# A four-layer image network on one core: start-up loads, the last experts and small vector work put elsewhere

## The chip, the cores and the metric

The kernel runs on one core of a Trainium2 chip. The metric is the device time of one execution in microseconds (us). The core has a tensor engine (PE, with its weight loads shown as PEld), a vector engine (DVE), an activation engine (ACT), GpSimd (POOL) and SyncE (SP), which issues DMAs. Each engine runs its own instructions in order and waits on semaphores where it needs another's result.

## The reference

The input is `x`, 4 images of 384 channels by 48 x 48 positions, in float32. Four layers follow one another, each `x = x + layer(group_norm(x))`:

```python
# layer 0: a Mamba block over the 2304 positions of an image, 768 inner channels, 16 states
xz = xs @ in_proj_w.T; xin, z = split(xz)
xin = silu(causal_conv4(xin) + conv_b)
dt, B, C = split(xin @ x_proj_w.T); dt = softplus(dt @ dt_proj_w.T + dt_proj_b)
h = exp(dt * A) * h + dt * B * xin        # per position, a scan; A = -exp(A_log)
y = (h * C).sum(states) + xin * D
out = layer_norm((y * silu(z)) @ out_proj_w.T) * gamma + beta
# layer 1: 1x1 product, an 8x8 patch FFT filter, a depthwise 3x3 convolution, a gelu gate, 1x1 product
# layer 2: a depthwise 11x11 convolution whose kernels are made from 4 points per channel
# layer 3: 4 experts (two 384x384 products with a relu), each weighted by a coefficient
present = (top_i[:, :, None] == arange(e)).any(0)     # is expert e anyone's k-th choice?
coef = einsum("ke,kbhw->ebhw", present, top_w)
out = einsum("ebohw,ebhw->bohw", y, coef)
```

If every expert is somebody's first and somebody's second choice, all coefficients are 1, and the last layer is the plain sum of the experts' outputs. The kernel computes that sum, works out from the gate scores whether the case holds (`route_all`), and has a second path (`weighted`) for the other case, which these inputs don't take.

## The kernel before, in words

The group normalisations are not applied to the data. Their scale goes into the weights of the product that follows (`fold` for layer 0, `begin` and `all_experts` for the experts), and the mean, multiplied by these weights, goes into a bias (the products with a right side one column wide, `pbias` and `pb`).

**Start.** Weights are loaded by `weight` (line 418) and a few direct calls, all issued on ACT's DMA queue. On SP's queue go three constants, then image 0, one channel tile of 128 x 2304 at a time, whose moments DVE takes by `bn_stats`, six to a tile (lines 477 to 481). `group_norm` makes mean and reciprocal deviation. Some small tables follow (`filt_t` by the product `fps`; `band`, layer 2's points as a matrix, made by DVE on lines 519 to 535), then `fold(0, 0)` and `fold(0, 1)` (x's half and z's half of the input weights), the load of the first chunk `xch`, which takes memory that the start's tiles held, and its products `pin`.

**Scans.** `scans` goes over 20 chunks (4 images of 5 chunks of about 460 positions), each of 96 slots. In a slot stands one scan over one channel tile and one state (`scan`, line 844), with its decay on ACT (`decay`), its drive on POOL (`drive`), the product with C on DVE or, in every third slot, on POOL, and the sum over states as transposes into PSUM on PE (`turned`, line 770). The whole order of this stage is written out (`manual_schedule`).

All other work is put beside these scans as tasks: generators whose every `yield` names an engine and may name a condition. A `Lane` holds tasks and moves each by one step in a slot; `Meter` lets only so much tensor work into a slot. `aux` holds layer 0's own work, placed by `plan` at slots given in numbers (`put(66, ...)`); `one` holds layers 1 to 3 of the image before (`later`), and `two` the experts of that image (`experts`), 16 blocks of 144 positions for each of 4 experts. A block is two groups of nine matrix products (`ph`, `pout`) with a relu on ACT between and an addition on DVE behind. Once in a chunk, at slot 64, `gates` runs Silu over a whole chunk for x and z, with a change of ACT's tables before and after it; the decays of later slots wait behind that. `image_stats` takes the moments of the next image in halves of three `bn_stats`. In layer 1 the depthwise convolution is 27 taps on DVE for each of 6 strips of an image, in `finish_strip`, two to three in a slot.

**Tail.** After the last scan, `one` runs layers 1 to 3 of the last image while `two` finishes the experts of the image before. Then `route_all` works the routes out of all scores, a chain of some 50 small DVE operations, and `all_experts` runs the four experts on the last image with all their weights in memory: it loads and scales the weights, makes the biases by `pb`, and goes over 16 blocks of positions. Outside the written-out stage a scheduler may move instructions past one another where the data allow it.

Of the kernel before, what the change touches and what calls it, by code (L numbers as in the profile page):

```python
# [9 lines left out]
F32 = mybir.dt.float32  # L10
# [129 lines left out]
def tile_layers(ctx: ExitStack, tc: tile.TileContext, a: dict, out: bass.AP):  # L140
# [272 lines left out]
    with ExitStack() as first:  # L413
        wp = first.enter_context(tc.tile_pool(name="weights", bufs=1))
        x1d = [dram.tile([C, HW], F32, name=f"x1d{b}") for b in range(NB)]
        x2d = [dram.tile([C, HW], F32, name=f"x2d{b}") for b in range(NB)]

        def weight(name, shape, src):
            t = wp.tile(shape, F32, name=name)
            nc.scalar.dma_start(t, src)  # L420
            return t
# [6 lines left out]
        conv_s = wp.tile([P, MT], F32, name="conv_s")  # L428
        nc.vector.tensor_reduce(conv_s, conv_w, AX.X, ALU.add)

# [4 lines left out]
        w_dt = wp.tile([DTR + 1, DI], F32, name="w_dt")  # L435
        nc.scalar.dma_start(w_dt[:DTR, :], a["L0_dt_proj_wT"])
        nc.scalar.dma_start(w_dt[DTR : DTR + 1, :], a["L0_dt_proj_b"].unsqueeze(0))
        a_neg = weight("a_neg", [P, MT, DS], per_channel(a["L0_A_log"]))
        nc.scalar.activation(a_neg, a_neg, AF.Exp)
        nc.vector.tensor_scalar_mul(a_neg, a_neg, -1.0)  # L440
        w_out0 = weight("w_out0", [P, MT, C], per_channel(a["L0_out_proj_wT"]))
# [21 lines left out]
        for e in range(NE):  # L463
            nc.scalar.dma_start(b1_all[:, e, :], column(a["L3_b1"][e]))
            nc.scalar.dma_start(b2_all[:, e, :], column(a["L3_b2"][e]))
        b2_sum = wp.tile([P, CT], F32, name="b2_sum")
        nc.vector.tensor_reduce(b2_sum, b2_all.rearrange("p e c -> p c e"), AX.X, ALU.add)

# [3 lines left out]
        with (  # L472
# [69 lines left out]
        edges = [sum(BANDS[:k]) for k in range(len(BANDS) + 1)]  # L542

        ordered = [False]

# [9 lines left out]

        def scans(wk, mm, ring, meter, place, lanes, begin):

# [24 lines left out]
            def fold(b, which):  # L582
                w = (w_inx, w_inz)[which]
                d = batch[b]
                nc.sync.dma_start(
                    w, per_channel(a["L0_in_proj_wT"])[:, :, bass.ts(which, DI)]
                )
                yield from wait(5)
# [389 lines left out]
            def plan(i, at):  # L978
# [9 lines left out]
                if i:  # L988
# [59 lines left out]
            now(fold(0, 0))  # L1048
            now(fold(0, 1))
            now(load(0))  # L1050
# [65 lines left out]
        def slow_slot():  # L1116
            return place[0] % (2 * DS) % 3 == 0

        def later(b, ring, accr):
# [124 lines left out]
            def finish_strip(hb):  # L1244
# [7 lines left out]
                def taps(ct):  # L1252
                    yield ("dve", 0, (accr, 1))
                    acc, k = sums[ct] = accr.take(f"dw{b}_{hb}_{ct}")
                    v = acc[:, :LB].rearrange("p (h w) -> p h w", w=W)
                    room = 3 if slow_slot() else 2
                    for k in range(9):
                        if not room:
                            yield ("dve",)
                            room = 3 if slow_slot() else 2  # L1260
                        room -= 1
# [277 lines left out]
        def experts(b, ring, rings):  # L1539
# [54 lines left out]
            def block(s, e):  # L1594
# [68 lines left out]
        def all_experts(b, wk, banks):  # L1663
# [25 lines left out]
            )  # L1689
            xs, hs, o = {}, {}, {}  # L1690

            def load3(s):
# [45 lines left out]
            for i, (s, e) in enumerate(order):  # L1738
# [9 lines left out]
        place = [0]  # L1748

# [35 lines left out]
        with (  # L1785
# [3 lines left out]
            holder[0] = mm  # L1789
            scans(wk, mm, ring, meter, place, [one, two], begin)  # L1790
            held, two.queue = two.queue, []
            at = place[0]
            while not all(ring.read):
# [6 lines left out]
        with (  # L1800
# [3 lines left out]
            holder[0], ring.n, accr.n = mm, 6, 2  # L1804
            of_experts(wk, {"we": 2, "xe": 3, "ye": 3, "hr": 3})

            one.queue += later(NB - 1, ring, accr)
            while one.queue or one.active or two.queue or two.active:
                at += 1
                meter.slot(0.0)  # L1810
                if not (one.queue or one.active):
                    meter.value = 0.0
                for act in (True, False):
                    for lane in (one, two):
                        lane.step(act, at)
            coef, whole = route_all(rt, mm)
            all_experts(
                NB - 1, wk,
                lambda tag, name: mm.tile(
                    [P, 512], F32, name=name, tag=tag, bufs=6 if tag == "mm" else 2  # L1820
                ),
            )

# [112 lines left out]
```

## Time and profile before

| what | us |
|---|---|
| median of 3 runs (5466.89 to 5471.5) | 5467.04 |
| the profiled execution | 5472.59 |
| its span | 5470.3 |
| first scan begins at | 88.66 |
| PE busy | 4689.8 |
| DVE busy | 4176.4 |
| POOL busy | 3124.6 |
| ACT busy | 2999.9 |

The costliest groups on the page (line, engine, operation, out<-in, count, busy us and mean ns, idle time ahead and its cause):

```profile
L844 DVE TENSOR_TENSOR_SCAN da<-da,carry,bu 128x460 f32<-128x460 f32 (+1 forms) x1008 | 1182.5, 1173 | 69.9 <-ACT da L820 48.7
L864 DVE TENSOR_TENSOR g<-da,C 128x460 f32<-128x460 f32 (+1 forms) x1260 | 796.4, 632 | 87.1 <-DMA C<-bcd 28.1
L1601 PE MATMUL pout<-hr,we 128*128 128x144 f32 x3456 | 488.9, 298 | 49.7 <-ACT hr L1617 30.5
L1266 DVE SCALAR_TENSOR_TENSOR dw<-pad,w_dw,dw 128x384 f32<-128x384 f32 x576 | 347.6, 614 | 17.4 <-ACT pad L1241 6.5
```

How to read it: PE shows two records for each float32 product. Busy time is an average over stages with different limits, so a stage's own row (busy time of each engine within it) says more than a share of the whole. A wait is put down to what came last. Idle time of an engine that isn't the bottleneck costs nothing.

### The profile page before, as it was taken

To read this page: it belongs to the slowest core of one execution; us is meant where nothing else is said; L and a number is where in the kernel's file an instruction comes from. 1 tells how busy PE (TensorE), PEld (TensorE's weight loads), DVE (VectorE), ACT (ScalarE), POOL (GpSimd) and SP (SyncE) were. 2 spreads that over 40 slices of the span, in tenths; PEclk is the share of its full clock that TensorE was granted. 3 is DMA by queue.
4 is the path that set the end of the run, shared out by engine and by line. 5 is a ranking of instruction groups with operands and counts; after the bars stand their busy time and mean duration, and the time that the engine had idled before them with its cause. 6 is when DMAs were issued, how large, how long until landed. Compare 5 with 4: busy or idle time off the path is not lost. (4 is left out here: it accounts for less than half of the span.)

```text
span 5470.3 us, 82006 instructions
## 1 busy us (share of the span) xinstructions
PE 4689.8 (86%) x27796; PEld 3688.4 (67%) x27796; DVE 4176.4 (76%) x5806; ACT 2999.9 (55%) x6632; POOL 3124.6 (57%) x2795
## 2 busy tenths in 40 slices
PE   5677677777678989988899999988899999999899
PEld 3445445454447767665678887665678878888799
DVE  5889989999898898899988788899988774443200
ACT  3555555565458765655467655665566753334321
POOL 3878878865567777665567667665666662000000
PEclk8788888798789999999899999999999999999899
DMA  4445445454345555544566566554556564543200
GB/s 121 135 137 147 124 128 146 128 149 124 104 125 148 151 160 163 172 140 140 152 169 174 155 166 175 153 154 130 164 158 169 163 175 145 148 138 102 66 27 23
DMA packets 628393, 758.97 MB, mean 139 GB/s; under 512 B 58869, under 2 KB 622181, under 8 KB 627582
## 3 DMA queue, kind: packets, MB, share of 16 engines
q1 hardware_dynamic: 617668, 751.98, 48.5%
q8 instruction: 221, 3.62, 0.3%
q10 hardware_dynamic: 10298, 1.67, 0.2%
q14 instruction: 206, 1.69, 0.1%
HBM read 663.81 MB, written 89.65 MB: 138 GB/s over the span
## 5 line engine op out<-in xcount | busy, mean ns | idle before, releaser
L831 POOL TENSOR_TENSOR bu<-u,B 128x460 f32<-128x460 f32 (+1 forms) x1920 | 2226.4, 1168 | 1118.2 <-DVE g L844 506.7
L820 ACT ACTIVATE da<-dt,a_neg 128x460 f32<-128x460 f32 (+1 forms) x1920 | 1243.7, 649 | 317.3 <-DVE g L864 223.0
L770 PE MATMUL y<-ident,g 128*115 128x128 f32 (+1 forms) x7680 | 1169.0, 295 | 273.4 <-DVE g L864 202.0
L770 PEld LDWEIGHTS y<-ident,g 128*115 128x115 f32 (+1 forms) x7680 | 1024.1, 185 | 546.9 <-DVE g L864 246.8
L844 DVE TENSOR_TENSOR_SCAN da<-da,carry,bu 128x460 f32<-128x460 f32 (+1 forms) x1008 | 1182.5, 1173 | 69.9 <-ACT da L820 48.7
L873 POOL TENSOR_TENSOR g<-g,C 128x460 f32<-128x460 f32 (+1 forms) x660 | 767.7, 1163 | 197.9 <-ACT carry L858 195.9
L864 DVE TENSOR_TENSOR g<-da,C 128x460 f32<-128x460 f32 (+1 forms) x1260 | 796.4, 632 | 87.1 <-DMA C<-bcd 28.1
L844 DVE TENSOR_TENSOR_SCAN g<-da,carry,bu 128x460 f32<-128x460 f32 (+1 forms) x528 | 616.8, 1168 | 105.6 <-ACT da L820 61.1
L858 ACT COPY carry<-da 128x1 f32<-128x1 f32 x1008 | 159.0, 158 | 948.1 <-DVE g L864 944.8
L1601 PE MATMUL pout<-hr,we 128*128 128x144 f32 x3456 | 488.9, 298 | 49.7 <-ACT hr L1617 30.5
L1601 PEld LDWEIGHTS pout<-hr,we 128*128 128x128 f32 x3456 | 461.1, 199 | 70.2 <-ACT hr L1617 40.6
L1601 PE MATMUL ph<-xe,we 128*128 128x144 f32 x3456 | 471.1, 292 | 15.2 <-DMA xe<-x3d 10.1
L1601 PEld LDWEIGHTS ph<-xe,we 128*128 128x128 f32 x3456 | 448.6, 195 | 30.4 <-DMA xe<-x3d 8.9
L1408 PE MATMUL pc<-band,row 128*128 128x162 f32 (+14 forms) x3456 | 456.2, 285 | 7.1 <-ACT row L1395 7.1
L1408 PEld LDWEIGHTS pc<-band,row 128*128 128x128 f32 x3456 | 443.5, 195 | 11.0 <-ACT row L1395 8.3
L642 PE MATMUL pin<-xch,w_inx 128*128 128x463 f32 (+2 forms) x720 | 332.5, 602 | 33.4 <-DMA xch<-in_x 20.0
L1266 DVE SCALAR_TENSOR_TENSOR dw<-pad,w_dw,dw 128x384 f32<-128x384 f32 x576 | 347.6, 614 | 17.4 <-ACT pad L1241 6.5
L915 PE MATMUL po<-w_out,zs 128*115 128x384 f32 (+1 forms) x960 | 342.4, 497 | 9.3 <-DVE dt L750 7.8
L674 PE MATMUL pinz<-xch,w_inz 128*128 128x460 f32 (+1 forms) x720 | 326.3, 592 | 0.3 <-DVE ye L1633 0.3
L1617 ACT ACTIVATE hr<-ph,nb 128x144 f32<-128x144 f32 x576 | 176.2, 376 | 268.2 <-PE ph L1601 267.8
L844 DVE TENSOR_TENSOR_SCAN da<-da,nil,bu 128x460 f32<-128x460 f32 x252 | 294.8, 1170 | 12.8 <-ACT carry L858 8.5
L1375 ACT ACTIVATE rep<-x,br,wr 128x192 f32<-128x192 f32 x576 | 274.1, 540 | 21.0 <-DVE br L1345 20.9
(202 smaller groups left out, 5725.4 us busy)
## 6 DMA issues: line engine op xcount, KB each, us to landing
B<-bcd SPq DMA_DIRECT2D x768, 230.0 KB, 3.5
C<-bcd SPq DMA_DIRECT2D x768, 230.0 KB, 3.8
B<-bcd SPq DMA_DIRECT2D x192, 232.0 KB, 3.7
C<-bcd SPq DMA_DIRECT2D x192, 232.0 KB, 4.0
xe<-x3d SPq DMA_DIRECT2D x192, 216.0 KB, 2.9
ye<-y3d SPq DMA_DIRECT2D x144, 216.0 KB, 2.8
y3d<-ye SPq DMA_DIRECT2D x96, 216.0 KB, 2.2
xs<-x1d SPq DMA_DIRECT2D x24, 576.0 KB, 4.9
```

The costliest lines, as they stand in the source:

```text
L642: nc.tensor.matmul(ps[:, lo : halo + n], lhsT=w_inx[:, k, bass.ts(j, P)], rhs=c["x"][:, k, lo : halo + n], start=k == 0, stop=k == CT - 1,)
L674: nc.tensor.matmul(ps[:, :n], lhsT=w_inz[:, k, bass.ts(j, P)], rhs=c["x"][:, k, DCONV - 1 : DCONV - 1 + n], start=k == 0, stop=k == CT - 1,)
L770: nc.tensor.matmul(c["y", m][:w, bass.ts(k, P)], lhsT=src[:, bass.ts(k, w)], rhs=ident, is_transpose=True, start=c["terms", m] == 1 and k ...
L820: nc.scalar.activation(da[:, :n], c["dt", p][:, m % 2, :n], AF.Exp, scale=a_neg[:, m, s : s + 1])
L831: nc.gpsimd.tensor_mul(bu[:, :n], c["u", p][:, m % 2, :n], live["B", u // 2][:, :n])
L844: nc.vector.tensor_tensor_scan(here[:, :n], da[:, :n], bu[:, :n], last if t else nil[:, 0:1], ALU.mult, ALU.add,)
L864: nc.vector.tensor_mul(live["g", u][:, :n], live["h", u][:, :n], live["C", u // 2][:, :n])
L873: nc.gpsimd.tensor_mul(g[:, :n], g[:, :n], live["C", u // 2][:, :n])
L915: nc.tensor.matmul(ps[:w, :C], lhsT=c["zs"][:, m, bass.ts(k, w)], rhs=w_out0[:, m, :], start=m == 0, stop=m == MT - 1,)
L1266: nc.vector.scalar_tensor_tensor(v, src, w_dw[:, ct, k : k + 1], v, ALU.mult, ALU.add)
L1408: nc.tensor.matmul(d["acc2"][0][:, : BANDS[k] * W].rearrange("p (h w) -> p h w", w=W)[:, lo - edges[k] : hi - edges[k], xlo:xhi], lhsT=d[" ...
L1601: nc.tensor.matmul(ps[:, bass.ts(m, EB)], lhsT=w[:, k, bass.ts(m, P)], rhs=of[:, k, :], start=k == 0, stop=k == CT - 1,)
```

## The change

Six things are done at once.

1. **Start.** `weight` and the other calls only note the loads. Image 0 goes first on SP's queue, in half tiles, then x's input weights, then all noted loads, now on SP's queue too. The sums and the exponential that need loaded weights stand behind the image's moments. z's weights are loaded, scaled and multiplied by the mean no longer before the first chunk but as a task at slot 4 of it.
2. **Moments.** The second half of each moments task is loaded from slot 56 on, not 66, and its three `bn_stats` go together into the gate's slot or the one after it.
3. **Taps.** In these two slots five taps may go, not two or three.
4. **Expert results.** In `experts`, one slot more lies between the second group of products and DVE's addition.
5. **Last experts.** `all_experts` becomes a generator in parts: all eight weight loads at the start of the tail; scaling, `pb` and bias when lane `one` is empty; 4 of the 16 blocks; then `route_all`; then the rest.
6. **Held tasks.** The last 24 tasks of lane `two` (a load and a block each) wait until lane `one` is empty.

```diff
+        loads = []
         def weight(name, shape, src):
             t = wp.tile(shape, F32, name=name)
-            nc.scalar.dma_start(t, src)
+            loads.append((t, src))
             return t
...
-                nc.sync.dma_start(t, a["x"][0, bass.ts(ct, P), :])
+                for h in range(2):
+                    part = bass.ts(h, HW // 2)
+                    nc.sync.dma_start(t[:, part], a["x"][0, bass.ts(ct, P), part])
                 for k in range(6):
                     nc.vector.bn_stats(stats0[:, 0, ct, k // 3, k % 3, :], t[:, bass.ts(k, LB)])
+            nc.sync.dma_start(w_inx, per_channel(a["L0_in_proj_wT"])[:, :, :DI])
+            for t, src in loads:
+                nc.sync.dma_start(t, src)
+            nc.vector.tensor_reduce(conv_s, conv_w, AX.X, ALU.add)
+            nc.scalar.activation(a_neg, a_neg, AF.Exp)
+            nc.vector.tensor_scalar_mul(a_neg, a_neg, -1.0)
+            nc.vector.tensor_reduce(b2_sum, b2_all.rearrange("p e c -> p c e"), AX.X, ALU.add)
...
+        def gated():
+            return gated_at[0] <= place[0] <= gated_at[0] + 1
...
                 yield from wait(6)
+                if h:
+                    yield ("dve", 0, None, lambda: gated())
                 for k in range(3):
-                    yield ("dve",)
+                    if not h:
+                        yield ("dve",)
                     nc.vector.bn_stats(stats0[:, b % 2, ct, h, k, :], t[:, bass.ts(k, LB)])
...
             def gates(i, j):
                 yield ("act",)
+                gated_at[0] = place[0]
...
+                if i == 0:
+                    put(4, ("fold", 0, 1), lambda: fold(0, 1))
...
-                            put(66, ("stats", b, t, 1), lambda: image_stats(b + 1, t, 1),
+                            put(56, ("stats", b, t, 1), lambda: image_stats(b + 1, t, 1),
...
             now(fold(0, 0))
-            now(fold(0, 1))
             now(load(0))
...
+        def room_for_taps():
+            return 5 if gated() else 3 if slow_slot() else 2
...
                 if s == NS - 1:
                     done(("w", e))
+                yield from wait(1)
                 yield ("dve",)
...
             for e in range(NE):
                 nc.sync.dma_start(w1[:, e], per_channel(a["L3_w1T"][e]))
                 nc.sync.dma_start(w2[:, e], per_channel(a["L3_w2T"][e]))
+            yield
+            for e in range(NE):
                 for k in range(CT):
                     nc.scalar.activation(
                         w1[:, e, k, :], w1[:, e, k, :], AF.Copy, scale=rstd3[:, b, k : k + 1]
                     )
...
             xs, hs, o = {}, {}, {}
+            yield
...
                 if i:
                     output(*order[i - 1])
+                if (s, e) == (4, 0):
+                    yield
             output(*order[-1])
+            yield
...
-            at = place[0]
+            at = place[0] + 1
...
+            last = all_experts(
+                NB - 1, wk,
+                lambda tag, name: mm.tile(
+                    [P, 512], F32, name=name, tag=tag, bufs=6 if tag == "mm" else 2
+                ),
+            )
+            next(last)
             one.queue += later(NB - 1, ring, accr)
+            ended = False
             while one.queue or one.active or two.queue or two.active:
                 at += 1
                 meter.slot(0.0)
                 if not (one.queue or one.active):
                     meter.value = 0.0
+                    if not ended:
+                        ended = True
+                        next(last)
+                held = [] if ended else two.queue[-24:]
+                two.queue = two.queue[: len(two.queue) - len(held)]
                 for act in (True, False):
                     for lane in (one, two):
                         lane.step(act, at)
+                two.queue += held
+            next(last)
             coef, whole = route_all(rt, mm)
-            all_experts(...)
+            next(last)
```

More of the change, by code (lines that the diff above doesn't have):

```diff
@@ L428, in tile_layers @@
         conv_s = wp.tile([P, MT], F32, name="conv_s")
-        nc.vector.tensor_reduce(conv_s, conv_w, AX.X, ALU.add)
         w_x = weight("w_x", [P, MT, XR], per_channel(a["L0_x_proj_wT"]))
@@ L435, in tile_layers @@
         w_dt = wp.tile([DTR + 1, DI], F32, name="w_dt")
-        nc.scalar.dma_start(w_dt[:DTR, :], a["L0_dt_proj_wT"])
-        nc.scalar.dma_start(w_dt[DTR : DTR + 1, :], a["L0_dt_proj_b"].unsqueeze(0))
+        loads.append((w_dt[:DTR, :], a["L0_dt_proj_wT"]))
+        loads.append((w_dt[DTR : DTR + 1, :], a["L0_dt_proj_b"].unsqueeze(0)))
         a_neg = weight("a_neg", [P, MT, DS], per_channel(a["L0_A_log"]))
-        nc.scalar.activation(a_neg, a_neg, AF.Exp)
-        nc.vector.tensor_scalar_mul(a_neg, a_neg, -1.0)
         w_out0 = weight("w_out0", [P, MT, C], per_channel(a["L0_out_proj_wT"]))
@@ L463, in tile_layers @@
         for e in range(NE):
-            nc.scalar.dma_start(b1_all[:, e, :], column(a["L3_b1"][e]))
-            nc.scalar.dma_start(b2_all[:, e, :], column(a["L3_b2"][e]))
+            loads.append((b1_all[:, e, :], column(a["L3_b1"][e])))
+            loads.append((b2_all[:, e, :], column(a["L3_b2"][e])))
         b2_sum = wp.tile([P, CT], F32, name="b2_sum")
-        nc.vector.tensor_reduce(b2_sum, b2_all.rearrange("p e c -> p c e"), AX.X, ALU.add)
         stats0 = wp.tile([P, 2, CT, 2, 3, 6], F32, name="stats0")
@@ L542, in tile_layers @@
         edges = [sum(BANDS[:k]) for k in range(len(BANDS) + 1)]
+        place = [0]
+        gated_at = [-9]
+        def gated():
+            return gated_at[0] <= place[0] <= gated_at[0] + 1
         ordered = [False]
@@ L554, in now, with scans @@
                 pass
-        def scans(wk, mm, ring, meter, place, lanes, begin):
+        def scans(wk, mm, ring, meter, lanes, begin):
             G = [(b, t) for b in range(NB) for t in range(NC)]
@@ L584, in fold @@
                 d = batch[b]
-                nc.sync.dma_start(
-                    w, per_channel(a["L0_in_proj_wT"])[:, :, bass.ts(which, DI)]
-                )
+                if b or which:
+                    nc.sync.dma_start(
+                        w, per_channel(a["L0_in_proj_wT"])[:, :, bass.ts(which, DI)]
+                    )
                 yield from wait(5)
@@ L1255, in taps @@
                     v = acc[:, :LB].rearrange("p (h w) -> p h w", w=W)
-                    room = 3 if slow_slot() else 2
+                    room = room_for_taps()
                     for k in range(9):
@@ L1259, in taps @@
                             yield ("dve",)
-                            room = 3 if slow_slot() else 2
+                            room = room_for_taps()
                         room -= 1
@@ L1743, in all_experts @@
                     output(*order[i - 1])
+                if (s, e) == (4, 0):
+                    yield
             output(*order[-1])
+            yield
         rings = {}
         holder = [None]
-        place = [0]
         def of_experts(pool, sizes):
@@ L1789, in tile_layers @@
             holder[0] = mm
-            scans(wk, mm, ring, meter, place, [one, two], begin)
+            scans(wk, mm, ring, meter, [one, two], begin)
             held, two.queue = two.queue, []
-            at = place[0]
+            at = place[0] + 1
             while not all(ring.read):
@@ L1805, in tile_layers @@
             of_experts(wk, {"we": 2, "xe": 3, "ye": 3, "hr": 3})
+            last = all_experts(
[3 more added lines that the diff above has]
+                ),
+            )
+            next(last)
             one.queue += later(NB - 1, ring, accr)
+            ended = False
             while one.queue or one.active or two.queue or two.active:
@@ L1815, in tile_layers @@
                         lane.step(act, at)
+                two.queue += held
+            assert ended
+            next(last)
             coef, whole = route_all(rt, mm)
[L1817 to L1822, printed above, removed]
+            next(last)
         flag = nc.values_load(whole[0:1, 0:1], min_val=0, max_val=1)
```

## The prediction

> **What bounds the kernel now.** I read the page first, then busy time by stage (windows cut where the first scan starts, where a layer's work begins, and at the tail), then the vector engine's waits, then the timelines of start and tail.
>
> ```profile
> PE 4689.8 (86%) x27796; PEld 3688.4 (67%) x27796; DVE 4176.4 (76%) x5806; ACT 2999.9 (55%) x6632; POOL 3124.6 (57%) x2795
> 88.00:1250.00 1162.00, 842.70 (x3744) 569.86 (x3745) 1053.02 (x1309) 673.20 (x1424) 941.74 (x841) 0.82 0.48 136
> 2700.00:3400.00 700.00, 667.25 (x4415) 552.61 (x4414) 581.12 (x779) 452.12 (x996) 473.36 (x417) 0.97 0.60 168
> 3900.00:4545.00 645.00, 607.01 (x4094) 506.77 (x4093) 524.23 (x683) 415.56 (x922) 432.31 (x381) 0.97 0.60 170
> ...
> 4559.00:4985.00 426.00, 406.35 (x2734) 352.20 (x2732) 177.74 (x354) 123.79 (x304) 3.19 (x12) 0.98 0.48 138
> 5123.90:5180.70 56.80, 35.55 (x159) 23.28 (x159) 15.95 (x56) 9.93 (x19) 0.54 (x1) 0.72 0.22 67
> 5180.70:5470.30 289.60, 283.90 (x2305) 283.68 (x2305) 17.79 (x62) 59.31 (x193) 0.00 (x0) 0.99 0.09 24
> ...
> DVE ye L1633 <- PE pout L1601: 85.4, 56, 3.8
> DVE g L844 <- ACT da L820: 67.2, 21, 8.2
> ...
> DVE xe L1636 <- PE pout L1601: 15.4, 15, 2.6
> ...
> 32.28 0.42 DVE L535 TENSOR_TENSOR band<-band,insidex 128x252 f32<-128x252 f32 x1
> 32.84 0.37 SPq L624 DMA_DIRECT2D xch<-in_x  x1
> ...
> 55.82 0.27 ACT L651 ACTIVATE pin<-nil,wm 128x3 f32<-128x3 f32 x1 [16.68 <-PE pin L642]
> ...
> 5164.90 0.59 PE L316 MATMUL pseen<-seen,ones 128*128 128x8 f32 x2 [12.89 <-DVE seen L310]
> 5165.34 15.50 PE L1678 MATMUL pb<-mean,w 128*128 128x1 f32 x72
> 5180.70 6.06 PE L1701 MATMUL ph<-xf,w 128*128 128x144 f32 x36
> ```
>
> A stage line gives length, then busy time of PE, PEld, DVE, ACT, POOL, clock share, DMA share, GB/s. The first scan stage is DVE's (1053.02 of 1162, 91%); where experts run beside scans it is PE's (95% and 94%). After the scans (about 4559 to 5470.3, 911 us) PE is the bound but for 5123.9 to 5180.7, where it is busy 35.55 of 56.8 us. The wait lines (total, times, longest; scans alone, 88 to 4540) show two kinds of DVE idleness that the change touches: the gates (ACT spends 1.28 + 2.50 + 2.49 + 1.28 = 7.5 us on table loads and Silu, and scans wait for `da`), and expert results not yet there (85.4 + 15.4 us).
>
> **What the Trainium skill says.** "TensorE: Matmul & The Clock Gate", part 1 on the HAM clock gate: half clock is the default, full clock needs a busy window of about 3.4 us, an idle one takes it back. The trace agrees: 72 passes of `pb` took 15.50 us at 5165 (0.215 each) after 12.89 us of waiting, 18 at 2316 took 2.09 us (0.116). "DMA: Bandwidth & Descriptors", "Anatomy of one DMA": [...]waits on semaphores are done by the issuing sequencer, so one blocked issue holds all behind it; the trace has a median of 2.4 us for the 1.5 KB `b_all` loads, and `xch` issued only 0.14 us after `band` ended. Same page, "Queues, rings and completion order": descriptors are consumed in ring order; no stage here shows eight large loads ahead of urgent ones, so that part is an estimate.
>
> **The change, part by part** (against the profiled span, 5470.3 us; that execution took 5472.59, the median of the runs shown is 5467.04, so a difference on the span is put on 5467).
>
> *Image first, z later.* Image data arrives at about 400 GB/s in both. Before, `a_neg` (issued at 4.38 us, used at 16.84) stood in DVE's order amid the moments, which ended at 22.4; with the weights behind, moments end near 14.5, 8 us earlier. But in the new instruction order 25 loads and 14 small ones stand on SP's queue ahead of `xch`, at 0.42 to 0.5 us an issue, each reusing the completion slot of the eighth before it; `w_out` waits for `w_inx` (about 15.5 us), `w_gate` for `w_out` (about 20.5), so `fsel` lands near 28.5. `fps` is ahead of x's bias products on PE: they run 30.2 to 38.2 (before 36.26 to 43.2), `cb` ends at 39, and DVE makes `band` only afterwards, by 41.8. `xch` waits for `band`, as before, so it is issued 9 us later and lands at 46.8 (5 us, as the 576 KB `xs` takes 4.9). First `pin`, three cold pairs of 1.54 us: 51.6 instead of 55.82, since z's bias products (7 us of PE amid the first `pin`) are gone. Gain 4.2 us, ends -1 and +9. z's fold then falls on the first scans: three scalings hidden under ACT's slack; 36 passes, cold, 7.8 us of PE, with `nwm` one slot behind on DVE and the scans queued after it. The fold at 802 us, as cold, shows what that costs: `nwm` waited 4.22 us. Cost 4.5 (0 to 7). Sum: **0**.
>
> *Moments and taps at gates.* Nine second-half moment groups (3 x 0.533 = 1.6 us) move to the slot after a gate, where DVE idles about 5 us; 14.4 us in all. Their load goes from slot 66 to 56 and lands (4.9 us) before. Worth full value where DVE is the bound, less at the rest: -11. Taps: in the new order only one gate gets more (+3 taps, but its gap was 0.8 us), while another loses its five (3.1 us) because the work drifts. Together **-9** (-14 to 0).
>
> *One slot more before DVE takes an expert's result.* 77 of the 101 us of waits lie in the two stages where PE is 94 to 95% busy: there DVE only waits for something else. Of the remaining 24 us I take a quarter, **-6** (-24 to +3). The price is a PSUM bank held one slot longer: in the new order seven expert products (18 passes, 2.25 us each) and one fold (2 us) fall behind the last scan. That takes 18 us of PE from stages where PE is mostly the bound; I count **-14** there (-18 to -4) and **+18** in the tail.
>
> *Tail.* Routing leaves PE's path: `pb` follows the last score transpose at 5152.0 instead of 5165.3, still at full clock. Such narrow products do not hold it (the fold at 956 us slows after some 23 passes), so about 30 x 0.112 + 42 x 0.213 = 12.3 us: end at 5164.3 instead of 5180.7, **-16.4** (-21 to -12). The scaling stays on ACT beside the scores, as now (done at 5137.2). The eight weight loads (4.7 MB) now stand ahead of all tail loads, by 4625 us; at 400 GB/s 12 us in which experts get no data but for two blocks already there (9 us). PE already idles 6 us in that place; I add **+3** (0 to 10). The last 24 tasks (12 blocks, with one in flight 25 products, 56 us) move from under layer 1 of the last image to behind `pb`. Layer 1 keeps 13 to 16 products between strips, against 15 to 19, 30 us or more, where a strip's 27 taps need 27 x 0.61 = 16.5 us of DVE: covered but for about **+2**.
>
> Sum: 0 - 9 - 6 - 14 + 18 - 16.4 + 3 + 2 = **-22.4 us**, so 5467.0 - 22.4 = **5445**.
>
> **Rivals.** (1) *The extra slot frees much more*: PE idles 33 of 700 and 38 of 645 us in the expert stages, and if decoupling fills over half of it, that entry is -45, giving 5406. For it: the long total of those waits. Against: PE's own waits there are mostly on Silu, `hr` and DMA. (2) *It comes to nothing*: scans go at DVE's pace after all, so taking PE work away gives -4 and the slot gives 0, and the eight loads cost 10: 0 - 9 - 4 + 18 - 16.4 + 10 + 2 = about 0, 5467. For it: DVE is at 87% or more in most chunks that lose products. (3) *Slower*: layer 1 of the last image goes at its own chain's pace. Then 426 us do not shrink when 18 net products (25 held, 7 added) leave it, and the held ones are pure addition: +40 for what I cost at nothing, sum +17.6, 5485. It decides from 23 us on. For it: each strip is a long chain over ACT, DVE and PE, and its end is already uncovered (PE idles near 4980). Against: PE is 95% busy there and DVE 42%.
>
> **How the numbers follow.** Forecast 0.56, rivals 0.14, 0.17, 0.13. What a measurement can tell from no change is 0.2%, 11 us. Forecast's own range, from its parts, 5430 to 5460. Faster: 0.9 x 0.56 + 0.14 + a bit of rival 2 = 0.67; same: the rest of the forecast and most of rival 2, 0.18; slower: rival 3 and an edge of rival 2, 0.15. The range, 5405 to 5475, leaves out most of rival 3 and the edge of rival 1.
>
> **What would show it.** Right: first scan near 84 us with `xch` issued near 42; gates with three moments in the gap; fewer expert waits of DVE; seven products more after the last scan; `pb` right behind the score transposes, 11 to 13 us long; no routing wait on PE. Wrong: a first scan at 78 or 92; a gap of over 10 us on PE near 4630; layer 1 of the last image still 420 us long; the last scan still near 4551 us.

## The result, and the profile after

The changed kernel takes 5476.21 us (median of 20 runs, 5465.54 to 5487.94), the kernel before 5467.6 in the runs beside it. The ratio is 1.0016, with a 95% interval from 1.001 to 1.0023: 9 us more, where 22 less had been forecast. That is under the 0.2% which the prediction called no change, and just above its range.

The busy times of the whole span, on the page's first table, hardly differ from before (PE 4689.8, DVE 4176.4); the work is the same and only its place is another.

```profile
PE 4677.3 (85%) x27796; PEld 3684.2 (67%) x27796; DVE 4175.0 (76%) x5806; ACT 2996.3 (55%) x6632; POOL 3124.6 (57%) x2795
```

The stage table of the changed kernel, cut at the same events as before (columns as there). The seventh row is new: the held experts, behind `pb`.

```profile
88.00:1250.00 1162.00, 847.68 (x3779) 577.17 (x3780) 1053.99 (x1310) 674.79 (x1427) 940.48 (x840) 0.82 0.47 137
2700.00:3400.00 700.00, 656.37 (x4237) 534.32 (x4236) 585.43 (x776) 448.91 (x984) 476.07 (x420) 0.96 0.58 166
3900.00:4545.00 645.00, 611.27 (x4161) 514.91 (x4160) 530.75 (x692) 416.40 (x925) 437.55 (x385) 0.97 0.59 169
4547.70:4939.70 392.00, 363.33 (x2381) 308.68 (x2380) 171.34 (x346) 115.41 (x276) 3.20 (x12) 0.97 0.47 137
4939.70:5079.50 139.80, 133.04 (x1106) 132.01 (x1107) 21.14 (x41) 93.34 (x216) 0.54 (x1) 0.95 0.28 84
5079.50:5121.20 41.70, 33.90 (x158) 21.66 (x157) 4.33 (x18) 9.49 (x18) 0.53 (x1) 0.76 0.30 92
5121.20:5182.60 61.40, 58.81 (x453) 57.73 (x453) 19.95 (x53) 12.54 (x41) 0.00 (x0) 0.97 0.43 116
5182.60:5473.20 290.60, 284.61 (x2324) 284.39 (x2322) 17.36 (x60) 59.21 (x193) 0.00 (x0) 0.99 0.09 24
```

The last `y` product ends at 4547.7 instead of 4562.3, 14.6 us earlier (in these two profiles). From there to the end, the tail, it takes 925.5 us instead of 908.0. So the scans gained half of the 29 us forecast for them, and the tail gave back more than that: 17.5 us instead of 6.6.

DVE's waits within the scans, 88 to 4540 us (total, times, longest):

```profile
DVE da L863 <- ACT da L839: 79.9, 101, 3.3
DVE g L863 <- ACT carry L877: 56.7, 18, 8.2
DVE g L863 <- ACT da L839: 55.6, 31, 6.3
DVE da L863 <- ACT carry L877: 38.8, 33, 3.6
...
DVE ye L1657 <- PE pout L1624: 14.9, 14, 2.0
```

Before, three of them that the prediction does not show:

```profile
DVE g L844 <- ACT carry L858: 50.7, 13, 6.2
DVE da L844 <- ACT da L820: 50.5, 63, 3.2
...
DVE da L844 <- ACT carry L858: 25.3, 29, 2.2
```

The waits for expert results fell as expected (`ye` from 85.4 us in 56 waits). The four for the scans' own operands grew in sum, from 193.7 to 231.0 us, though `g` on `da` fell (67.2 before). About half of what stood behind an expert's product now stands behind something else.

The timeline of the start:

```profile
29.34 0.33 SPq L498 DMA_DIRECT2D fsel<-in_c_fsel  x1
31.36 1.62 PE L500 MATMUL fps<-fsrc,fsel 40*128 40x384 f32 x2 [9.97 <-DMA fsel<-in_c_fsel]
44.43 0.42 DVE L542 TENSOR_TENSOR band<-band,insidex 128x252 f32<-128x252 f32 x1
44.98 0.38 SPq L642 DMA_DIRECT2D xch<-in_x  x1
...
54.00 0.27 ACT L669 ACTIVATE pin<-nil,wm 128x3 f32<-128x3 f32 x1 [10.90 <-PE pin L660]
...
87.40 1.17 DVE L863 TENSOR_TENSOR_SCAN g<-da,nil,bu 128x460 f32<-128x460 f32 x1 [2.01 <-POOL bu L850]
```

`xch` waits for `band` and is issued 12 us later than before; the first scan is 1.3 us earlier. The routing has left PE's path: `pb` follows the last score transpose directly.

```profile
5106.71 0.34 PE L1541 MATMUL pgt<-ident,sc 4*128 4x4 f32 x3 [0.45 <-ACT sc L1535]
5106.98 14.26 PE L1704 MATMUL pb<-mean,w 128*128 128x1 f32 x72
5121.10 6.79 PE L1624 MATMUL ph<-xe,we 128*128 128x144 f32 x36
```

### The profile page after: what moved, and what is told of

Same layout as the page of the kernel before. It is cut to its first block, busy times and chain, and to the rows that moved or that the text cites. A ratio compares the mean times of both kernels' runs of the same rounds, so it can differ in the third digit from the quotient of the medians.

```text
span 5473.2 us, 82031 instructions
## 1 busy us (share of the span) xinstructions
PE 4677.3 (85%) x27796; PEld 3684.2 (67%) x27796; DVE 4175.0 (76%) x5806; ACT 2996.3 (55%) x6632; POOL 3124.6 (57%) x2795
## 5 line engine op out<-in xcount | busy, mean ns | idle before, releaser
L1624 PE MATMUL ph<-xe,we 128*128 128x144 f32 x3456 | 487.5, 298 | 42.6 <-DMA xe<-x3d 22.2
L1624 PEld LDWEIGHTS ph<-xe,we 128*128 128x128 f32 x3456 | 462.4, 200 | 60.7 <-DMA xe<-x3d 17.5
L660 PE MATMUL pin<-xch,w_inx 128*128 128x463 f32 (+2 forms) x720 | 333.6, 604 | 52.7 <-DMA xch<-in_x 14.7
```

The costliest lines, as they stand in the source:

```text
L660: nc.tensor.matmul(ps[:, lo : halo + n], lhsT=w_inx[:, k, bass.ts(j, P)], rhs=c["x"][:, k, lo : halo + n], start=k == 0, stop=k == CT - 1,)
L1624: nc.tensor.matmul(ps[:, bass.ts(m, EB)], lhsT=w[:, k, bass.ts(m, P)], rhs=of[:, k, :], start=k == 0, stop=k == CT - 1,)
```

## The experiments

Times are medians, and ratios are to the kernel before on the same chip, whose median was 5466.6, 5468.5, 5469.1, 5467.7 and 5469.2 us in the five sets. A single profile can be off by some 10 us over the scans: the last `y` of tail_only, whose scans are those of before, ends 11 us earlier than before's. The tail is steadier: 904 to 909 us in the seven kernels whose tail is that of before. So totals are taken from the medians, whose ratios are good to 4 to 8 us, and the profiles are read for where a difference lies. Chunks are compared from the first scan of one to the first of the next.

### Each part alone in the kernel before

**start_only**

```diff
-            nc.scalar.dma_start(t, src)
+            loads.append((t, src))
...
+            for t, src in loads:
+                nc.sync.dma_start(t, src)
...
+                    put(4, ("fold", 0, 1), lambda: fold(0, 1))
```

> The kernel before with only the start changed (image ahead of the weights on one queue, z's fold four slots into the scans). Theory P (the prediction's sum): 0 us, first scan near 84 us. Theory N (the parts give back what they gain): 0 to +4 us, xch issued near 45 us instead of 32.8, first scan near 87, and z's bias products standing in the first scans. Time P 5467, N 5467 to 5471.

5478.66 us, ratio 1.0019 (1.0012 to 1.0026): 12 us lost, where both theories had 4 at most. `xch` is issued at 44.92 and the first scan begins at 87.1, as theory N has it.

**gate_only**

```diff
+                if h:
+                    yield ("dve", 0, None, lambda: gated())
...
+            return 5 if gated() else 3 if slow_slot() else 2
```

> The kernel before with only the moments and taps put at the gates. Theory P: -9 us, 5458. Theory N: the gaps of the gates close by only about 1.3 us each, nine of them, and part of that comes back as other waits of DVE: -3 to -5 us, 5462 to 5464, scans of chunks 0 to 2 shorter by about 1.3 us each.

5485.64 us, 1.0033 (1.0021 to 1.0045). Both theories miss, in sign too: 19 us lost. Up to chunk 6 its profile is ahead of before's; chunks 7 to 9 are 23 us longer.

**slot_only**

```diff
+                yield from wait(1)
                 yield ("dve",)
                 key = ("y" if e else "x", s, e)
```

> The kernel before with only the one slot more between an expert's second product and DVE's taking of it. Seven products fall behind the last scan. Theory P: -6 -14 +18 = -2 us, 5465; last scan near 4531. Theory N: DVE's removed waits for pout come back as waits for the scans' own operands, so the scans gain only what the seven products took of PE, 8 us or less, and the tail grows by 15 to 18: +7 to +10 us, 5474 to 5477; last scan near 4543.

5450.86 us, 0.9969 (0.9958 to 0.9979): 16 us gained, far outside both. In the profile the last `y` ends 20.9 us earlier (11.2 in slot_and_tail, whose scans are the same), and the tail, with seven products more in it, is 905.1 us against 908.0.

**tail_only**

```diff
+            next(last)
...
+                held = [] if ended else two.queue[-24:]
+                two.queue = two.queue[: len(two.queue) - len(held)]
...
             coef, whole = route_all(rt, mm)
+            next(last)
```

> The kernel before with only the tail changed (last weights loaded and scaled early, pb ahead of routing, 24 tasks held back behind layer 1). Theory P: -16.4 +3 +2 = -11.4 us, 5456; layer 1 of the last image (last y to the last strip's pb) near 366 us against 421.8. Theory N: layer 1 shrinks by about 30 us less what the held products (26 of 2.25 us) cost behind it, so the hold loses 20 to 28 and the route and pb gain 16 to 20: 0 to +10 us, 5467 to 5477.

5492.02 us, 1.0049 (1.0035 to 1.0063): 25 us lost, the largest loss so far and outside both theories. Layer 1 of the last image did shrink, from 421.8 to 396.6 us, but behind `pb` 61.9 us of held experts follow. Within layer 1 PE now waits for the strips, 20.5 us where it was 1.9:

```profile
PE pb L1294 <- DVE act L1288: 20.5, 2, 10.6
```

### The gates taken apart

**moments_only** (`if h: yield ... gated()` and the load at slot 56) and **taps_only**:

```diff
-                    room = 3 if slow_slot() else 2
+                    room = room_for_taps()
```

> The kernel before with only the second half's moments put at the gates; TensorE's order is the one of before. Theory P: -11 us, 5456 (against 5466.6). Theory T (the loss of gate_only comes from the taps, whose drift brings 13.5 us of layer 2's products forward into chunks 7 to 9): -7 to -9 us here, 5458 to 5460, and no chunk longer than before. Theory M (the loss is the moments', which crowd the slots behind the gates where layer 1 or 2 is running): +15 us or more, 5482.

> The kernel before with only the taps' room at a gate changed (five where two or three were). Theory P: +2 us. Theory T: chunks 7 to 9 longer by 20 to 24 us together, 5486 to 5495. Theory M: within 3 us of before, 5464 to 5470.

moments_only: 5465.58, 0.9999 (0.9991 to 1.0007), nothing that can be told from none. taps_only: 5502.06, 1.0055 (1.0042 to 1.0068), 34 us lost. Theory T holds for the cause; its forecast for the moments was too good, and the one for the taps too small. At a gate itself the moments are free, as the timeline of DVE shows. Before:

```profile
206.51 1.16 DVE L844 TENSOR_TENSOR_SCAN g<-da,nil,bu 128x460 f32<-128x460 f32 x1
...
210.65 0.64 DVE L864 TENSOR_TENSOR g<-da,C 128x460 f32<-128x460 f32 x1
216.89 1.17 DVE L844 TENSOR_TENSOR_SCAN g<-da,nil,bu 128x460 f32<-128x460 f32 x1 [5.61 <-ACT carry L858]
```

In the changed kernel:

```profile
209.19 1.17 DVE L863 TENSOR_TENSOR_SCAN g<-da,nil,bu 128x460 f32<-128x460 f32 x1
...
211.34 1.45 DVE L590 BATCH_NORM_STATS2 stats<-xs 128x6 f32<-128x384 f32 x3
...
214.51 0.64 DVE L883 TENSOR_TENSOR g<-da,C 128x460 f32<-128x460 f32 x1
219.58 1.18 DVE L863 TENSOR_TENSOR_SCAN g<-da,nil,bu 128x460 f32<-128x460 f32 x1 [4.43 <-ACT carry L877]
```

From the scan shown first to the one behind the gap it takes 10.4 us in both. The gap shrinks by 1.2 us, which is what three moments in a row take of DVE's time (their records overlap their neighbours'), so nine such groups are 11 us at best. What that is worth depends on the slots that they leave. In chunks 1 and 2, where DVE is busy for 91% of the time, the eight kernels with the moments moved take 3.5 us less on average than the eleven others: the forecast's full worth of two groups. In chunks 5 to 7 and 10 to 12 moments_only is only 1.3 and 1.2 us below the mean of the six kernels whose order there is that of before.

The taps are more curious: one gate takes three taps more (chunk 6), and chunks 7 to 9 become longer. The stage rows of chunks 7 to 9 and 10 to 12, cut at the scans. Before:

```profile
1505.09:2147.79 642.70, 557.69 (x3281) 424.50 (x3281) 573.61 (x762) 427.91 (x900) 468.24 (x414) 0.92 0.52 149
2147.79:2905.51 757.72, 665.51 (x3825) 513.41 (x3826) 667.74 (x950) 437.71 (x1007) 470.41 (x422) 0.93 0.55 156
```

taps_only:

```profile
1501.67:2173.44 671.77, 588.75 (x3452) 456.25 (x3453) 574.25 (x775) 429.35 (x911) 469.54 (x415) 0.90 0.49 146
2173.44:2928.50 755.06, 662.73 (x3755) 511.05 (x3754) 663.08 (x937) 437.80 (x1003) 467.40 (x419) 0.93 0.54 156
```

Layer 2 starts 4 scans earlier and the experts behind it 21: 171 more passes of PE (the records that it shows, two for a product; 3452 less 3281) within the same 288 scans, all of them experts'. The stretch is 29.1 us longer (theory T had 20 to 24), PE's busy time 31.1, DVE's 0.6; PE's idle time, 85 us before, is 83. Chunks 7 to 9 take 665 to 672 us in all six kernels with the taps' edit and 637 to 650 in the thirteen others. By chunk 16 all that work has been given back in the order, and the time has not: chunks 13 to 19 have 100 passes fewer and are 10 us longer (1655.4 against 1644.9). Work pulled forward cost its full time; work then missing gave none back.

### The tail taken apart

**tail_no_hold** is tail_only with the lines of `held` removed; **slot_and_tail** is the same with `yield from wait(1)`.

> The kernel before with the tail's change but nothing held back: experts run under layer 1 as before, the last weights load early, pb stands ahead of the routing. Theory H (the 26 held products are nearly free under layer 1, and the hold alone makes the tail lose): pb right behind the last score transpose, -13 to -16 us, 5451 to 5454. Theory P (held products cost the same in both places): -11 us plus the early weights' +3, as with the hold: 5490 if the loads or the route are what costs in tail_only.

> The kernel before with one slot more ahead of DVE's taking of an expert's result, and the tail's change without the hold. Theory H: the two add up, -16 -14 = -30 us, 5437. Theory P: no better than the slot alone, 5451, because the seven products that fall into the tail leave nothing uncovered for the route to give.

tail_no_hold: 5463.18, 0.9991 (0.9983 to 0.9999), between its theories; slot_and_tail: 5449.46, 0.9963 (0.9949 to 0.9976), theory P's time. So the hold is what makes tail_only lose, but route and `pb` bring 5 us, not 15, and with the slot almost nothing. PE's waits in layer 1 of the last image (4551.1 to 4967.0) in slot_and_tail show why:

```profile
PE ph L1601 <- DMA xe<-x3d: 14.0, 2, 13.2
PE pout L1601 <- ACT hr L1617: 9.0, 18, 0.8
```

In slot_only the first of these is 2.9 us, and layer 1 takes 402.1 us against 415.9 here. The eight weight loads stand on the queue ahead of the experts' blocks, which theory P did not have in mind.

**slot_moments_late_tail** tests that: slot, moments and tail without hold, with the loads behind the layers.

```diff
+            yield
             for e in range(NE):
                 nc.sync.dma_start(w1[:, e], per_channel(a["L3_w1T"][e]))
                 nc.sync.dma_start(w2[:, e], per_channel(a["L3_w2T"][e]))
-            yield
-            for e in range(NE):
                 for k in range(CT):
```

> The kernel before with one slot more ahead of DVE's taking of an expert's result, the second half's moments at the gates, and routing behind pb; nothing held, the last weights loaded behind the layers as before. Theory H (the eight early loads were what took the route's gain in slot_and_tail): slot -16, moments -1 to -4, route and pb -13 to -15, together 5433 to 5438. Theory U (in the tail the seven extra products take the place of what the route gives): 5447 to 5451.

5430.54 us, 0.9933 (0.992 to 0.9946): theory H, 2 us below its range, and faster than both kernels. It has the moments too; its tail alone is 14 us shorter (888.8 against 902.6 us). Its wait for `xe` in layer 1:

```profile
PE ph L1612 <- DMA xe<-x3d: 1.8, 3, 0.8
```

### The start taken apart

**z_fold_only** moves only z's fold (`put(4, ...)`); **start_tables_first** has on SP's queue the image, x's input weights, two small loads and then the tables, and the other weights on ACT's queue, where they run beside the image again:

```diff
+            for t, src in loads[:2]:
+                nc.sync.dma_start(t, src)
...
+            for t, src in loads[2:]:
+                nc.scalar.dma_start(t, src)
```

> The kernel before with only z's fold put four slots into the scans; all loads as before. Theory P (the prediction's terms): first pin 2 to 4 us earlier, 4.5 us lost in chunk 0: within 3 us of before. Theory Z (z's 36 narrow products and its scalings in chunk 0 are the 6 to 12 us that start_only lost): 5473 to 5478, and chunks 0 and 1 longer by 4 us.

> The kernel before with the image first, z's fold four slots into the scans, but the tables that band and fps need ahead of the weights, and the weights on ACT's queue as before. Theory Q (SP's queue of 39 loads ate the gain of the early image): xch issued near 32 us, first pin near 38, first scan near 81, that is 6 us or more earlier than in the changed kernel; 5471 if z's fold costs what start_only lost. Theory B (another chain, band's or cb's on DVE, is no earlier anyway): first scan within 2 us of 87.

z_fold_only: 5464.72, 0.9997 (0.9989 to 1.0005), near theory P; its first scan is at 80.9, 7.8 us earlier than before, since x's bias products are no longer followed by z's. The fold then costs about what was forecast (4.5 us): chunk 0 takes 182.4 to 184.1 us in the seven kernels with it and 177.9 to 181.0 in the twelve without, 4.2 us less on average. start_tables_first: 5480.27, 1.0016 (1.0008 to 1.0024), first scan at 84.0. Both theories on it miss: `xch` was issued at 41.90, for `band` stood behind `cb` on DVE, and `cb` behind `fps` and `pbias` on PE. The loads were not the whole of it. (The image's moments end at 20.7 us here, at 15.6 in the changed kernel and at 22.4 before.) With the image ahead on SP's queue both kernels lose 11 to 12 us (9 to 10 by the ratios) though their first scan is 1.5 and 4.6 us earlier than before. Against z's fold alone it is 6.2 and 3.1 us later. Where the rest goes is not settled: start_only's chunks differ from z_fold_only's by no more than those of two profiles of one order do.

### Parts taken out of the changed kernel

**after_no_taps** has the old `room`, **after_no_hold** no `held`, **after_no_start** the old start.

> The changed kernel with only the taps' room set back to what it was before. Theory T (the taps' drift is the single largest loss of the change): chunks 7 to 9 shorter by 20 to 25 us than in the changed kernel, last scan near 4520, 5450 against 5476. Theory I (what the taps cost, the other parts give back whatever the taps do): 5470 or more.

> The changed kernel without the 24 held tasks. Theory H (the hold loses 25 to 30 us wherever it stands): 5446 to 5451 against 5476. Theory P (held products cost the same in both places): 5476 or more.

> The changed kernel with the start of before (weights on ACT's queue, z's bias ahead of the scans). Theory S (image first loses about 10 us everywhere, as in start_only and start_tables_first): 5464 to 5468. Theory N (it is lost in what follows): within 4 us of 5476.

after_no_taps 5468.85, 1.0001 (0.9993 to 1.001): 7 us better than the changed kernel, within the noise of theory I. Its chunks 7 to 9 are 25 us shorter, as theory T has it, but its chunks 13 to 19 are 20 us longer. after_no_hold 5450.76, 0.9964 (0.995 to 0.9977): 25 us better, theory H. after_no_start 5468.9, 1.0004 (0.9996 to 1.0013): 7 us better, a little less than theory S.

The tail of after_no_hold (layer 1; layer 2; scores and `pb`; the last image):

```profile
4552.70:4970.10 417.40, 391.81 (x2650) 340.54 (x2648) 175.60 (x352) 122.75 (x300) 3.19 (x12) 0.98 0.48 140
4970.10:5126.20 156.10, 155.04 (x1303) 153.43 (x1303) 24.61 (x47) 97.60 (x231) 0.54 (x1) 1.00 0.31 93
5126.20:5166.80 40.60, 33.38 (x158) 20.63 (x157) 4.34 (x18) 9.49 (x18) 0.53 (x1) 0.75 0.31 94
5166.80:5457.20 290.40, 284.44 (x2307) 284.22 (x2307) 29.78 (x100) 59.73 (x194) 0.00 (x0) 0.99 0.08 23
```

Here the 26 products are in layers 1 and 2, which take 573.5 us together; with them held it is 531.8, and 61.4 follow. Held, they cost 61.4 - 41.7 = 20 us more. Layers 1 and 2 had 35 us of idle PE without them and 27 with them, and PE's busy time there grew by only 50.5 us for 466 passes, where 453 behind `pb` take 58.8 and leave 2.6 us idle. So of the 20 us some 9 are gaps no longer filled, 8 are busy time that the passes take more by themselves, and 3 are new gaps.

### What the slot is worth, and why the taps cost less beside it

**products_out** moves eight products behind the last scan by another means:

```diff
-                yield ("pe", 2.2, (ring, 1), lambda: rings["hr"].free())
+                yield ("pe", 2.4, (ring, 1), lambda: rings["hr"].free())
...
-                yield ("pe", 2.2, (ring, 1))
+                yield ("pe", 2.4, (ring, 1))
```

> The kernel before with the weight of an expert's product in the meter 2.4 instead of 2.2: eight products fall behind the last scan, DVE takes a result as early as before. Theory M (what the slot gains is the work that leaves the scans for a tail that has room for it): -12 to -18 us, 5451 to 5457, with DVE's waits for pout still near 85 us. Theory W (the slot's gain is the removed waits of DVE): no gain, 5467 to 5475.

5486.69 us, 1.0036 (1.0024 to 1.0049): 19 us lost, more than theory W had (no gain), and the opposite of theory M: moving work behind the last scan does not gain by itself. With 18 us of PE less in the scans its last `y` ends 0.4 us later than before's, and its tail is 921.5 us long against 908.0. DVE's wait for results is still there (88 to 4540 us):

```profile
DVE ye L1633 <- PE pout L1601: 77.4, 49, 4.5
```

In slot_only it isn't (1490 to 4540 us, in which all such waits lie):

```profile
DVE ye L1634 <- PE pout L1601: 11.9, 13, 1.9
```

The two do not move the same products: the weight spaces all experts anew, and takes its eight mostly from chunks 13 to 15, the slot its seven mostly from chunks 10 to 12. So the place that they leave could be what counts. The rows of chunks 10 to 12 speak against that. In slot_only:

```profile
2149.68:2888.30 738.62, 651.62 (x3737) 502.30 (x3737) 663.29 (x948) 434.47 (x1000) 470.57 (x422) 0.93 0.54 157
```

That is 88 passes fewer than before and 19 us less. In taps_only it is 70 passes fewer and 3 us less. All nine kernels with the slot take 735 to 742 us there, the ten others 747 to 759. How the slot shortens these chunks isn't shown.

In the tail the slot helps again: layers 1 and 2 of the last image take 574.7 us in products_out and 558.2 in slot_only, which has one product less there. With the slot the experts run on for 30 us into layer 2 (6.5 in products_out), and PE idles 14 us in the two layers instead of 23.

**slot_and_taps** has both edits and nothing else.

> The kernel before with the one slot more and the taps' room at the gates, nothing else. Theory A (the two add): 5451 + 33 = 5484. Theory S (with the slot the products that the taps bring forward are put back by chunk 12 and not by chunk 15, so most of the taps' loss is returned): 5455 to 5462, chunks 7 to 9 longer by 20 to 25 us than in slot_only and chunks 10 to 12 shorter by 8 us or more.

5461.45 us, 0.999 (0.9982 to 0.9998): 11 us above the slot alone, not 34. The time is that of theory S, its way is so only in chunks 7 to 9:

```profile
1504.07:2171.73 667.66, 583.35 (x3408) 450.45 (x3409) 573.43 (x772) 428.38 (x908) 468.99 (x415) 0.90 0.49 146
2171.73:2910.59 738.86, 643.21 (x3656) 492.29 (x3655) 662.14 (x937) 431.62 (x990) 470.00 (x422) 0.93 0.54 157
2910.59:4551.90 1641.31, 1514.84 (x9667) 1226.17 (x9667) 1387.32 (x1878) 1022.68 (x2261) 1090.37 (x967) 0.96 0.56 161
```

Chunks 7 to 9 take 23.7 us more than in slot_only (643.95), chunks 10 to 12 the same (738.62), though with 81 passes fewer, and chunks 13 to 19 take 6 us less (1647.35) where with the taps alone they took 10 more. In all four kernels with both edits chunks 13 to 19 are shorter than in any of the five with the slot and without the taps. What makes the difference there isn't known.

**slot_moments_z** is slot_moments_late_tail with z's fold moved.

> slot_moments_late_tail with z's fold four slots into the scans and all loads as before. Theory A (the earlier first scan of z_fold_only, 8 us, reaches the end where nothing else is late): 5423 to 5427. Theory N (it is lost within the scans, as in z_fold_only's own time): 5428 to 5434.

5427.34 us, 0.9918 (0.9904 to 0.9931). The interval overlaps that of slot_moments_late_tail, so the 3 us between them are not shown, and the theories are not told apart. Both are faster than either kernel of this study.

## Why the prediction was wrong, step by step

Most of the mechanisms forecast are in the trace, and most of their sizes were wrong. Term by term, in us:

| term | forecast | measured | from |
|---|---|---|---|
| start | 0 | +7 | changed kernel less after_no_start; alone +12 |
| moments | -11 | -3, within -5 to +4 | moments_only |
| taps | +2 | +7 | changed kernel less after_no_taps; alone +34 |
| slot and the seven products | -6 -14 +18 = -2 | -16 | slot_only |
| route and `pb` | -16.4 | -14.7 | last score transpose to end of `pb`, 28.8 before, 14.1 after |
| eight weight loads | +3 | +11 to +14 | waits for `xe`; slot_and_tail against slot_only |
| layer 1 without the held products | +2 | +20 by profile, +25 by medians | after_no_hold |

With the middle of the loads' bounds and the profile's 20, the measured column adds up to +13, against a measured +9. Differences of two medians are good to some 6 to 8 us, and terms measured beside different neighbours need not add (the taps cost 34 alone and 7 here), so the sum agrees in size and proves no more.

- **"covered but for about +2"** is the step that failed most. It counted 56 us out of layer 1 and 56 us in behind `pb`, and looked only at the time between the strips. That was covered (PE waits 3.2 us for `act`). But taking the held products out of layers 1 and 2 gave 42 us back, and running them by themselves took 61. A good part of this lies just behind layer 1, where PE has nothing but the short chain of layer 2's normalisation, and where the experts run on if they are not held. These 13.5 us in the changed kernel, then in after_no_hold:

```profile
4939.70:4953.20 13.50, 6.74 (x37) 5.96 (x38) 2.71 (x11) 5.01 (x12) 0.54 (x1) 0.50 0.39 123
4970.10:4983.60 13.50, 13.50 (x113) 13.02 (x114) 3.94 (x11) 1.84 (x6) 0.10 (x1) 1.00 0.69 206
```

  Without the hold the changed kernel takes 5450.76 us, inside the forecast's own range of 5430 to 5460 (in part by luck, since the slot then makes up for the start, the gates and the loads). In the kernel before the experts ended ahead of layer 2 as well, so against it layer 1 shrank about as forecast (by 29.8 us; 56 - 18 - 3 - 2 = 33). What the hold took was what the slot had brought to the tail. Rival 3 named this place, with a price of 40 for layer 1's own chain; half of its price came, and its reason shows in tail_only (20.5 us), where the slot's seven products are missing.
- **"I add +3" for the loads.** The wait for `xe` is 13.6 us at 4623 us, where the longest was 4.4. The text had 12 us of transfer against 9 us of cover, then took 3; the gap of over 10 us near 4630 that it named as a sign of error came:

```profile
4622.81 4.57 PE L1624 MATMUL ph<-xe,we 128*128 128x144 f32 x18 [13.61 <-DMA xe<-x3d]
```

  The Trainium skill's page "DMA: Bandwidth & Descriptors", section "Queues, rings and completion order", has descriptors consumed in ring order on each DMA engine, and the prediction could only estimate what that does here. The waits agree with it, and these runs price eight large loads ahead of urgent ones at 11 to 14 us.
- **Start, "Sum: 0".** The parts were right in kind (`fsel` landed near 31.4, forecast 28.5; `xch` at 44.98, forecast 41.8; first scan at 87.4, forecast 84), z's fold costs its 4.5 us in chunk 0, and nothing of it can be told at the end (z_fold_only). What image-first loses behind the first scan was not foreseen and isn't explained.
- **Moments and taps, "-9".** The room in the gaps was free, as forecast, and in the first chunks the moments brought their full worth. What was too large is the worth put on the later chunks: by the medians a quarter of the 11 us reached the end. The taps were priced by what a tap takes, when what counted was the work that starts sooner behind them.
- **Slot, "-6 -14 +18".** In the scans the sum was near (forecast -20; the last `y` is 21 and 11 us earlier in two profiles), but by luck: the products' leaving, put at "-14", brought nothing (products_out), which leaves the gain to the waits, put at a quarter, although most of them did come back under other names. In the tail the "+18" failed: with seven products more it is 3 us shorter than before (slot_only), where eight cost 13.5 in products_out. As products_out loses 19 us in all, the slot itself is worth about 16 + 19 x 7 / 8 = 33 us, an estimate that takes the two as additive.
- **Route, -16.4.** Right; `pb` takes 14.3 us where 12.3 was forecast. The 15.50 us of `pb` before were read as agreeing with the clock rule that is quoted there. They agree that a long wait leaves a slow clock. But the 72 passes then stay at 0.215 us each for 15.5 us without a gap, far more than the 3.4 us quoted, so the rule fits only if such narrow products do not count as busy; no run here tests that.

Against the forecast the hold came out 18 us dearer, the loads 9, the start 7, the gates 13, the route 2, and the slot 14 cheaper: 35 us by the terms, where the total missed by 31.

## What to carry to other kernels

Work that fills the gaps of a stage costs less there than its own duration, and costs all of it when it is taken out and run by itself: before moving it, price it by the stage's length with and without it, and look at the ends of the stage, where other work may run dry. Pulling dependent work forward isn't free even where the receiving stage has idle time (chunks 7 to 9 grew by nearly all of it), and the stage it leaves may not become shorter. A bundle of edits that each look worth a few us has to be run edit by edit: here the image first, the taps, the early loads and the hold hid a slot that gains 16 us alone and 39 together with the moments and the route behind `pb`.

## What the runs showed of the hardware

- In layer 2 of the last image PE's granted clock was 0.95 with 1106 passes in 139.8 us (changed kernel) and 1.00 with 1303 in 156.1 (after_no_hold). The difference lies at the layer's start: 0.50 in the first 13.5 us, with PE busy for half of them, and 0.99 behind that. The 197 passes more cost 16 us, 0.08 us each, where held passes took 0.13.
- The 72 narrow passes of `pb` took 15.50 us in each of the ten kernels in which PE waits 12.9 us for the routing ahead of them. In the nine in which they follow the score transposes directly they took 11.73 to 14.42 us, without a gap in either case. What spreads the nine isn't known.
